# The tail of a graph network's layer 0 in chunks of 8, 4 and 10 tiles, with a table for each early place

## The chip, the cores and the metric

The kernel runs on one core of one Trainium2 chip. The metric is device time in microseconds (us) of a whole run. A core has five engines that run side by side, each with its own instructions in its own order: TensorE (PE, matrix products and transposes; PEld is its weight load), VectorE (DVE), ScalarE (ACT), GpSimd (POOL) and SyncE (SP), which only issues DMAs here. An engine waits for another one, or for a DMA, by a semaphore.

## The reference

Four graph layers over N = 2708 nodes with D = 128 features. The adjacency is sparse (8.0 neighbours a row on the mean) and all entries of one row are equal, so a row is known from one value and the places of its entries.

```
# layer 0: hyperbolic; every factor comes from row norms
h = h_add(h_mul(relu(layernorm(x)), embed), embed_bias)
neigh = exp_map_zero(adj @ log_map_zero(h))
x = x + h_add(h_mul(concat(relu(layernorm(x)), neigh), layer), layer_bias)
# layer 1: messages along edges
h = relu(layernorm(x));  s = h @ msg_w[:, :D].T;  d = h @ msg_w[:, D:].T
aggregated[i] = sum_j adj[i, j] * gelu(s[i] + d[j] + msg_b)
x = x + layernorm(gelu(concat(h, aggregated) @ upd_w.T + upd_b) + h) * ln_w + ln_b
# layers 2 and 3: products with adj and with weights
```

## The kernel before

**Tiles.** The nodes lie in T = 22 tiles of 128 (the last one has 20 rows), and the tiles in six blocks: 0 to 4 of four tiles, 5 of two. `first_half` is 12 tiles, blocks 0 to 2; the list `late` is blocks 3, 4 and 5.

**Layer 0.** For each block `read_block` loads a slab of the transposed adjacency in six pieces, and ACT makes a 0/1 mask of each (L999). From the masks come two things. The first is the product with all 22 tiles: 66 matmuls a block, three bf16 parts for each tile (`add_product`, L1324), and then the row norms (`end_product`, L1347). The second is the list of each row's neighbours: PE packs the mask into words (`words_in`, L1028, L1046), DVE takes the 24 largest words of a row (`find_words`, L1057 to L1072) and decodes them (`find_columns`), and POOL fetches one value for each row by an indirect DMA for each tile (L1120, `val`). `lay_out` sorts the neighbours of a half of the tiles into places: EARLY = 2 early places, HEAD - EARLY = 4 head places, and the rest into packed tail lists of NQ = 3 chunks a tile.

**The tail of layer 0** is a chain through small instructions: `neighbours` (row factors, the product with the layer's weights at L948, the sum at L1375, squares on ACT at L1383), then `update` (`norm`, `log_factor` and `moebius` on one column per tile, with two ACT table loads at L865 and L883; the new x at L1403 and L1408; `normal_form`, whose last instruction is returned as `formed`; then for each block h on ACT at L926, its transpose at L936, the product d with `msg_w` at L948, a copy to `v` at L1421 and DMAs to DRAM at L1424). It runs twice: for blocks 0 to 2, and for blocks 3 to 5. d goes to two tables in DRAM: `d_early` with the first 12 tiles' rows, and `d_hbm` with all.

**Order.** The framework orders each engine's instructions by their place in the program and by its own estimate of when each is ready. `queue_behind(ins)` adds an order by hand: an instruction stays behind `ins` on its engine. So the transposes of the first `update` stand behind the first 12 matmuls of product 4 (`last`), and the other 54 behind the last d matmul (`latest["times"]`); `find_words` of blocks 4 and 5 stands behind `formed`.

**The gathers.** POOL issues indirect DMAs that fetch a row of d for each of 128 nodes. `gather_early` (L1523) fetches both early places of 21 tiles, 42 gathers: a place whose neighbour is among the first 12 tiles reads `d_early`, and a miss is put with the tail. Its buffers are the three that the adjacency pieces used. `mark_edges` (L1237, L1240) and `pack_edges` (L1260 to L1306, one batch for each block, all behind the last d matmul) make the tail lists' indices `tail_c`.

**Layer 1's loop.** `prelude(g)` makes the node's own rows s (into `v`) and the update's own part for four tiles, and splits s into three bf16 parts (`split`, L783 to L786). Row t of the loop, `messages`, gathers 4 head places (`g`) and 3 tail chunks (`gt`, both L1727, from `d_hbm`, 4 buffers each), adds s, takes Gelu, sums on PE (L1787, L1789) and goes on to layer 1's end and layer 2's product (L1645). `prelude(0)` stands before the loop; the others go into its first rows. On-chip pools are stacked: `words`, `left`, `wide0`, `small` and others are closed before the loop, and the loop's pools lie where they lay.

Of the kernel before, what the change touches and what calls it, by code (L numbers as in the profile page):

```python
# [42 lines left out]
P = 128  # L43
# [513 lines left out]
def sparse_stack(  # L557
# [169 lines left out]

    d_hbm = dram.tile([NP + 1, D], F32, name="d_hbm")
    d_early = dram.tile([first_half * P + 1, D], F32, name="d_early")
# [18 lines left out]
    def load_later():  # L748

        nc.gpsimd.dma_start(out=d_hbm[NP : NP + 1, :], in_=none)  # L750
        nc.gpsimd.dma_start(out=d_early[first_half * P :, :], in_=none)
        for w, src in (
            (msg_w, msg_wt),
            (upd_w, upd_wt),
            (w2_w, w2),
            (self_w, w_self),
            (neigh_w, w_neigh),
        ):
            nc.gpsimd.dma_start(out=w, in_=src.rearrange("(a p) o -> p a o", p=P))
        for r, src in ((msg_br, msg_b), (upd_br, upd_b), (ln_wr, ln_w), (ln_br, ln_b)):  # L760
            nc.gpsimd.dma_start(out=r, in_=src.partition_broadcast(P))
# [25 lines left out]


# [7 lines left out]
    with ExitStack() as st:  # L796
# [14 lines left out]
        for t in range(T):  # L811
            nc.gpsimd.tensor_scalar_mul(shifts[:, t, :], ident, float(2 ** (T - 1 - t)))

# [22 lines left out]
        place = wide.tile([P, P], I32, name="place")  # L836
# [120 lines left out]
        def times_bias(w, bias, out, name):  # L957

            ps = ps_one.tile([P, BANK], F32, tag="one", name=f"wt{name}")
            nc.tensor.transpose(ps[:, :P], w, ident)  # L960
            wT = pair_p.tile([P, P], F32, tag="wT", name=f"wT{name}")
            nc.vector.tensor_copy(wT, ps[:, :P])
            nc.tensor.matmul(ps[:, P : P + 1], wT, bias, start=True, stop=True)
            nc.vector.tensor_copy(out, ps[:, P : P + 1])
# [57 lines left out]
        def pack(b):  # L1022
# [4 lines left out]
            for t in range(T):  # L1027
                nc.tensor.matmul(  # L1028
                    pk[:, :w], shifts[:, t, :], mask[:, t, sl], start=(t == 0), stop=(t == T - 1)
                )  # L1030
            return pk

        def words_in(b):
# [5 lines left out]
            pk = pack(b)  # L1039
# [87 lines left out]

        def lay_out(sl):
# [5 lines left out]
            from_c = float((T - first_half + 1) * P)  # L1134
# [4 lines left out]
            nc.vector.tensor_scalar(near, first[:, :, :EARLY], from_c, None, op0=ALU.is_ge)  # L1139
            nc.vector.scalar_tensor_tensor(  # L1140
                cand[:, sl, 2, SLOTS - EARLY :],
                first[:, :, :EARLY],
                from_c,
# [7 lines left out]
                -(from_c + first_half * P),  # L1151
# [4 lines left out]
            if sl.stop < T:  # L1156
                nc.vector.tensor_scalar_add(early_c[:, sl, :], miss, float(first_half * P))
# [92 lines left out]
        def pack_edges(b, after):  # L1250

            t0, t1 = blocks[b]
            n = t1 - t0
            px = ps_one.tile([P, BANK], F32, tag="one", name=f"ex{b}")
            px = px[:, : n * NQ * 32].rearrange("p (t q c) -> p t q c", t=n, c=32)
            for k in range(n):
                t = t0 + k
                for q in range(NQ):
                    with queue_behind(after):
                        nc.tensor.matmul(  # L1260
                            px[:, k, q, : TAIL + 3],
                            r_all[:, t, q * P : (q + 1) * P],
                            edge_x[:, t, :] if q < tails(t) else short_x,
                            start=True,
                            stop=True,
                        )
            ex = small.tile([P, BLOCK, NQ, TAIL + 3], F32, tag="ex", name=f"exs{b}")
            nc.scalar.copy(ex[:, :n], px[:, :, :, : TAIL + 3])  # L1268
            m = n * NQ
            kth, past, jump = (  # L1270
                small.tile([P, BLOCK * NQ], F32, tag=name, name=f"{name}{b}")[:, :m]
                for name in ("kth", "past", "jump")
            )
            flat_ex = ex.rearrange("p t q c -> p (t q) c")[:, :m, :]
            edge = small.tile([P, BLOCK, NQ], F32, tag="edge", name=f"edge{b}")[:, :n, :]
# [3 lines left out]
                tail_r[:, t0:t1, :].rearrange("p t q -> p (t q)"), flat_ex[:, :, TAIL + 2]  # L1279
            )  # L1280

            nc.vector.tensor_sub(kth, edge, flat_ex[:, :, TAIL])
            nc.vector.tensor_tensor(past, edge, flat_ex[:, :, TAIL + 1], ALU.is_ge)
            nc.vector.tensor_sub(jump, flat_ex[:, :, TAIL], flat_ex[:, :, TAIL + 1])
# [4 lines left out]
            sel = small.tile([P, BLOCK * NQ, TAIL], F32, tag="sel", name=f"sel{b}")[:, :m, :]  # L1289
# [6 lines left out]
            nc.vector.tensor_mul(sel, sel, flat_ex[:, :, :TAIL])  # L1296
            cf = small.tile([P, BLOCK * NQ], F32, tag="cf", name=f"cf{b}")[:, :m]
            nc.vector.tensor_reduce(cf, sel, AX.X, ALU.add)
            nc.vector.tensor_scalar_add(
                tail_c[:, t0:t1, :].rearrange("p t q -> p (t q)"), cf, MID  # L1300
            )
            if t1 == T:
                q = (n - 1) * NQ + tails(full)
                nc.vector.tensor_mul(sel[:, q, :HEAD], is_place, flat_ex[:, q, :HEAD])
                nc.vector.tensor_reduce(cf[:, q : q + 1], sel[:, q, :HEAD], AX.X, ALU.add)
                nc.vector.tensor_scalar_add(  # L1306
                    tail_c[:, full, tails(full) : tails(full) + 1], cf[:, q : q + 1], MID
                )
# [47 lines left out]
        def neighbours(bs, sums):  # L1356
# [3 lines left out]
            nc.vector.tensor_mul(n_sq, sums[0][:, : sl.stop - sl.start], val[:, sl])  # L1360
# [9 lines left out]
            for t0 in range(sl.start, sl.stop, 3):  # L1370
                g = slice(t0, min(t0 + 3, sl.stop))
                ps = tiles_times(g, yT, layer_w[:, 1, :], f"ne{t0}")
# [19 lines left out]
        def update(bs, copy, after):  # L1392
# [22 lines left out]
            for b in bs:  # L1415
# [6 lines left out]
                for table, end in ((d_early, first_half), (d_hbm, T)):  # L1422
# [96 lines left out]
        def gather_early(ts):  # L1519
            for t in ts:  # L1520
                n = rows(t)
                for k in range(EARLY):
                    nc.gpsimd.indirect_dma_start(  # L1523
                        out=early_d[t // EACH][:n, t % EACH, k, :],
                        out_offset=None,
                        in_=d_early,
                        in_offset=bass.IndirectOffsetOnAxis(ap=early_c[:n, t, k : k + 1], axis=0),
# [4 lines left out]
        sums = sums_of([0, 1, 2])  # L1532
# [10 lines left out]
        end_product(1, acc, sums)  # L1543
        lay_out(halves[0])
        with queue_behind(scaled):
            nc.vector.tensor_scalar(
                spread[:, : HEAD * rest].rearrange("p (k r) -> p k r", r=rest), apart, 0.0, None,
                op0=ALU.is_equal, saturate=False,
# [5 lines left out]
        find_words(3, words_in(3))  # L1554
        find_columns(groups[3])
        read_block(4)
        product(2, sums)
        neighbours([0, 1, 2], sums)
        read_block(5)
        sums = sums_of(late)  # L1560
        product(3, sums)
        words = {b: words_in(b) for b in (4, 5)}
        acc = begin_product(4)
        split_at = BLOCK
        last = add_product(4, acc, range(split_at))
        formed = update([0, 1, 2], nc.scalar.copy, last)
        find_words(4, words[4], formed)
# [5 lines left out]
        add_product(4, acc, range(split_at, T), latest["times"])  # L1573
# [4 lines left out]
        gather_early(range(first_half))  # L1578
# [5 lines left out]
        with queue_behind(last):  # L1584
            nc.vector.tensor_scalar_add(
                early_c[:, halves[1], :], late_c, float(first_half * P)
            )
        gather_early(range(first_half, full))
# [3 lines left out]
        for b in range(nb):  # L1592
            pack_edges(b, latest["times"])
# [98 lines left out]

    group_p = held.enter_context(tc.tile_pool(name="group", bufs=3))
    with ExitStack() as st_m:
        hot_p = st_m.enter_context(tc.tile_pool(name="hot", bufs=3))
        gath_p = st_m.enter_context(tc.tile_pool(name="gath", bufs=4))
        small = st_m.enter_context(tc.tile_pool(name="small1", bufs=2))
        junk_p = st_m.enter_context(tc.tile_pool(name="junk", bufs=1))

        def prelude(g):  # L1700

            sl = groups[g]
            n = sl.stop - sl.start
            for t in range(sl.start, sl.stop, 2):
                two = slice(t, min(t + 2, sl.stop))
                m = two.stop - t
                ps = ps_one.tile([P, BANK], F32, tag="one", name=f"own{t}")
                ps = ps[:, : m * 2 * D].rearrange("p (n j d) -> p n j d", j=2, d=D)
                for k in range(m):
                    nc.tensor.matmul(  # L1710
                        ps[:, k, :, :],
                        hT[:, (t + k) * P : (t + k + 1) * P],
                        pair_w[:, 0::2, :],
                        start=True,
                        stop=True,
                    )
                nc.vector.tensor_add(v[:, two, :], ps[:, :, 0, :], row_of(msg_br, m))
                left = group_p.tile([P, 2, D], F32, tag="left", name=f"lefts{t}", bufs=2)
                last = nc.vector.tensor_add(tmp[:, two, :], ps[:, :, 1, :], row_of(upd_br, m))
                split(v, two, left[:, :m, :])  # L1720
            with queue_behind(last):
                nc.vector.tensor_add(x[:, sl, :], x[:, sl, :], row_of(ln_br, n))
            return last
# [120 lines left out]
        first = prelude(0)  # L1844
# [5 lines left out]
        for t0, t1 in zip(starts, starts[1:] + [T]):  # L1850
# [3 lines left out]
            for k in range(n):  # L1854
# [6 lines left out]
                if begun < len(groups):  # L1861
                    prelude(begun)
# [194 lines left out]
```

## Time and profile before

| what | us |
|---|---|
| median of 3 runs | 555.48 (555.25 to 558.63) |
| the profiled execution, the whole run | 556.43 |
| its span | 554.6 |
| PE, DVE, ACT, POOL busy | 422.5, 419.9, 236.6, 234.7 |
| first early gather issued | 166.68 |
| last d copied to `v` | 204.19 to 204.56 |
| first head gather of the loop issued | 222.69 |
| last tail gather of the loop issued | 412.4 |

All times inside the span count from its start. An engine that is busy for three quarters of the span may still not set its end: layer 0 is mostly PE and DVE work, and the loop in the middle has POOL issuing gathers, so the stretches have to be read one by one. The busy shares of the page are for matmuls, vector work and POOL's indirect DMAs; issuing by SP isn't counted.

### The profile page before, as it was taken

To read this page: it belongs to the slowest core of one execution; us is meant where nothing else is said; L and a number is where in the kernel's file an instruction comes from. 1 tells how busy PE (TensorE), PEld (TensorE's weight loads), DVE (VectorE), ACT (ScalarE), POOL (GpSimd) and SP (SyncE) were. 2 spreads that over 40 slices of the span, in tenths; PEclk is the share of its full clock that TensorE was granted. 3 is DMA by queue.
4 is the path that set the end of the run, shared out by engine and by line. 5 is a ranking of instruction groups with operands and counts; after the bars stand their busy time and mean duration, and the time that the engine had idled before them with its cause. 6 is when DMAs were issued, how large, how long until landed. Compare 5 with 4: busy or idle time off the path is not lost.

```text
span 554.6 us, 8223 instructions
## 1 busy us (share of the span) xinstructions
PE 422.5 (76%) x2504; PEld 262.1 (47%) x2504; DVE 419.9 (76%) x1743; ACT 236.6 (43%) x570; POOL 234.7 (42%) x268
## 2 busy tenths in 40 slices
PE   0981999999993062276877968879877999989994
PEld 0760354464753051265646644646553555445652
DVE  6977986767998989437679786879546599998742
ACT  2867966766424131324535434454534344300100
POOL 8800022220047777777777777777760000000000
PEclk9996899999998555668888987989997999999998
DMA  8893779970031132123146473752220250399011
GB/s 260 278 318 124 227 248 331 305 210 2 1 115 43 52 96 52 48 52 104 51 151 203 153 206 101 232 170 52 54 47 2 83 219 1 116 390 394 20 57 51
DMA packets 39332, 77.89 MB, mean 140 GB/s; under 512 B 5754, under 2 KB 18614, under 8 KB 37722
## 3 DMA queue, kind: packets, MB, share of 16 engines
q1 hardware_dynamic: 30270, 63.15, 33.1%
q0 software_dynamic: 7264, 13.40, 9.6%
q10 hardware_dynamic: 1744, 0.72, 0.5%
q8 instruction: 22, 0.36, 0.3%
q14 instruction: 32, 0.26, 0.1%
HBM read 73.63 MB, written 3.62 MB: 139 GB/s over the span
## 4 chain that ended last, share of the span: by engine, by line
PE 37%; DVE 31%; DMA 12%; POOL 6%; issue 6%; ACT 5%; ACTq 0%; DVEq 0%
PE three L1645 8%; PE acc L1324 8%; PE two L1645 7%; DMA gt<-d_hbm,tail_c 5%; DMA a<-in_adj_t_dram 4%; POOL g L1727 4%; DVE eq L1661 3%; POOL gt L1727 3%; PE msg L1787 3%; DMA layer_w<-in_L_gnn_layer_dram 2%; PE d L948 1%; DMA hT<-in_adj_dram 1%; PE pk L1028 1%; DVE mask L994 1%; PE neigh L1684 1%
## 5 line engine op out<-in xcount | busy, mean ns | idle before, releaser
L1645 PEld LDWEIGHTS <-parts 128*128 128x128 bf16 x792 | 75.3, 101 | 90.4 <-issue 9.5
L1645 PE MATMUL two<-mask,parts 128*128 128x512 fp8e4 (+1 forms) x396 | 88.8, 381 | 9.3 <-ACT parts L1630 5.1
L1727 POOL DMA_INDIRECT g<-d_hbm,head_c x84 | 82.9, 986 | 25.8 <-issue 22.6
L1324 PE MATMUL acc<-mask,parts 128*128 128x512 fp8e4 (+1 forms) x396 | 79.6, 355 | 0.7 <-DVE parts L786 0.4
L1645 PE MATMUL three<-mask,parts 128*128 128x512 fp8e4 (+1 forms) x396 | 79.0, 354 | 0.6 <-ACT parts L1630 0.5
L1727 POOL DMA_INDIRECT gt<-d_hbm,tail_c x65 | 62.7, 964 | 19.8 <-issue 15.2
L1120 POOL DMA_INDIRECT val<-in_adj_dram,ai x22 | 22.0, 998 | 104.5 <-DVE left L1108 91.3
L1324 PEld LDWEIGHTS <-parts 128*128 128x128 bf16 x396 | 36.6, 98 | 47.6 <-ACT parts L783 7.5
L1523 POOL DMA_INDIRECT early<-d_early,early_c x42 | 43.0, 1023 | 12.8 <-issue 11.9
L999 ACT ACTIVATE mask<-a 128x2048 fp8e4<-128x2048 uint32 (+3 forms) x27 | 38.2, 1434 | 10.0 <-DMA a<-in_adj_t_dram 9.8
L1661 DVE TENSOR_SCALAR_CACHE_REDUCE eq<-row,val 128x2708 fp8e4<-128x2708 f32 (+1 forms) x13 | 39.4, 3031 | 2.4 <-DMA row<-in_adj_dram 2.3
L1028 PE MATMUL pk<-mask,shifts 128*128 128x512 fp8e4 (+1 forms) x132 | 31.1, 372 | 13.0 <-ACT mask L999 12.4
L1740 PE MATMUL msg<-parts,r_all 128*128 128x128 bf16 x195 | 15.7, 227 | 19.0 <-DVE u L1804 13.7
L1661 DVE TENSOR_SCALAR_CACHE_REDUCE eq<-hT,val 128x1354 fp8e4<-128x1354 f32 x18 | 29.1, 1619 | 0.1
L1787 PE MATMUL msg<-ident,early 128*128 128x128 f32 x84 | 16.4, 327 | 16.6 <-DVE gt L1776 13.3
L1776 DVE TENSOR_TENSOR gt<-gt,msg 128x384 f32<-128x384 f32 (+1 forms) x22 | 12.0, 545 | 21.5 <-DMA gt<-d_hbm,tail_c 19.1
L1710 PE MATMUL own<-pair_w,hT 128*128 128x256 f32 x44 | 15.9, 503 | 13.6 <-ACT exs L1268 9.6
L1787 PE MATMUL msg<-ident,g 128*128 128x128 f32 x168 | 25.5, 302 | 0.0
L926 ACT ACTIVATE h<-x,n_nb,n_rstd 128x128 f32<-128x128 f32 x44 | 18.2, 486 | 17.0 <-DVE n_nb L920 17.0
L1787 PEld LDWEIGHTS msg<-ident,g 128*128 128x128 f32 x168 | 24.2, 221 | 0.2
L1740 PEld LDWEIGHTS <-r_all 128*128 128x128 fp8e4 x195 | 13.5, 102 | 22.1 <-issue 18.0
L1773 DVE TENSOR_TENSOR g<-g,v 128x512 f32<-128x512 f32 x21 | 14.5, 689 | 11.3 <-DMA g<-d_hbm,head_c 11.3
(407 smaller groups left out, 867.2 us busy)
## 6 DMA issues: line engine op xcount, KB each, us to landing
a<-in_adj_t_dram SPq DMA_DIRECT2D x25, 1024.0 KB, 7.6
row<-in_adj_dram SPq DMA_DIRECT2D x12, 1354.0 KB, 9.6
hT<-in_adj_dram SPq DMA_DIRECT2D x18, 677.0 KB, 4.1
a<-in_adj_t_dram SPq DMA_DIRECT2D x5, 296.0 KB, 4.9
g<-d_hbm,head_c POOLq DMA_INDIRECT x84
a<-in_adj_t_dram SPq DMA_DIRECT2D x5, 256.0 KB
d_hbm<-v SPq DMA_DIRECT2D x5, 256.0 KB, 3.7
out_dram<-x SPq DMA_DIRECT2D x5, 256.0 KB
```

The lines of the kernel that those rows point to most:

```text
L926: nc.scalar.activation(h[:, t, :], x[:, t, :], AF.Relu, bias=node("nb")[:, t : t + 1], scale=node("rstd")[:, t : t + 1],)
L999: nc.scalar.activation(mask[:, g : g + n, sl], bits[:, :n, :w], AF.Sign, saturate=False)
L1028: nc.tensor.matmul(pk[:, :w], shifts[:, t, :], mask[:, t, sl], start=(t == 0), stop=(t == T - 1))
L1120: nc.gpsimd.indirect_dma_start(out=val[:, t : t + 1], out_offset=None, in_=flat, in_offset=bass.IndirectOffsetOnAxis(ap=ai[:, t : t + 1], ...
L1324: last = nc.tensor.matmul(acc[:, :w], parts[:, t, k, :], mask[:, t, sl], start=(t == 0 and k == 0), stop=(t == T - 1 and k == 2),)
L1523: nc.gpsimd.indirect_dma_start(out=early_d[t // EACH][:n, t % EACH, k, :], out_offset=None, in_=d_early, in_offset=bass.IndirectOffsetOnAx ...
L1645: last = nc.tensor.matmul(accs[b][:, : sl.stop - sl.start], parts[:, t, k, :], mask[:, t, sl], start=(t == 0 and k == 0), stop=(t == T - 1 ...
L1661: last = nc.vector.tensor_scalar(eq[:n, : c1 - c0], a, val[:n, t : t + 1], None, op0=ALU.is_equal, op1=ALU.add, accum_out=same[:n, t, k : ...
L1710: nc.tensor.matmul(ps[:, k, :, :], hT[:, (t + k) * P : (t + k + 1) * P], pair_w[:, 0::2, :], start=True, stop=True,)
L1727: nc.gpsimd.indirect_dma_start(out=g[:n, q, :], out_offset=None, in_=d_hbm, in_offset=bass.IndirectOffsetOnAxis(ap=table[:n, q : q + 1], a ...
L1740: nc.tensor.matmul(ps[:, q * D : (q + 1) * D], r_all[:, t, q * P : (q + 1) * P], parts[:, t, k, :], start=(k == 0), stop=(k == 2),)
L1787: nc.tensor.matmul(sums, part, ident, start=(q == 0), stop=False)
```

## The change

It does four things.

1. **Three chunks instead of two.** `neighbours` and `update` run for blocks 0 and 1 (8 tiles), for block 2 (4 tiles) and for `late` (10 tiles). The order of layer 0's tail is rewritten around this: product 3's first 12 matmuls go ahead of the first `update`'s transposes and its other 54 behind that update's last d matmul; the packing of words 4 and 5 goes behind product 3; product 4 is cut in the same way around `update([2])`.
2. **A table for each early place.** `reach` is [8 tiles, 12 tiles]. The first early place reads `d_early[0]`, the second `d_early[1]`. `lay_out` compares with a constant for each place (`from_c`, `none_c`). The 12 gathers of the first place for the first half are issued after `update([0, 1])`, the 12 of the second after the last values' gathers, and the 18 of the late tiles as before.
3. **Edges' packing in four batches**, blocks [0], [1, 2], [3, 4] and [5], with `prelude(0)` between the first and the second. `prelude` becomes a function of the whole kernel.
4. **Pools.** `gath` (buffers of `g` and `gt`) moves to the bottom of the loop's stack, ahead of `group`; `place` is allocated behind `shifts`; `wT` uses a `left` buffer.

```
+    reach = [groups[1].stop, first_half]
+    d_early = [dram.tile([n * P + 1, D], F32, name=f"d_early{n}") for n in reach]
...
+            nc.vector.tensor_tensor(near, first[:, :, :EARLY], each(from_c, n), ALU.is_ge)
...
-                for table, end in ((d_early, first_half), (d_hbm, T)):
+                for table, end in ((d_early[0], reach[0]), (d_early[1], reach[1]), (d_hbm, T)):
...
+        def times_layer(bs):
+            sl = slice(blocks[bs[0]][0], blocks[bs[-1]][1])
+            return {
+                t0: tiles_times(
+                    slice(t0, min(t0 + 3, sl.stop)), yT, layer_w[:, 1, :], f"ne{t0}"
+                )
+                for t0 in range(sl.start, sl.stop, 3)
+            }
...
-        sums = sums_of([0, 1, 2])
+        sums = sums_of([0, 1])
...
         end_product(1, acc, sums)
+        neighbours([0, 1], sums)
+        words = {3: words_in(3)}
+        read_block(4)
+        sums = sums_of([2])
+        product(2, sums)
+        times = times_layer([2])
+        acc = begin_product(3)
+        last = add_product(3, acc, range(BLOCK))
+        formed = update([0, 1], nc.scalar.copy, last)
+        through = latest["times"]
         lay_out(halves[0])
...
-        find_words(3, words_in(3))
+        neighbours([2], sums, formed, times)
+        find_words(3, words[3])
         find_columns(groups[3])
-        read_block(4)
-        product(2, sums)
-        neighbours([0, 1, 2], sums)
         read_block(5)
-        sums = sums_of(late)
-        product(3, sums)
-        words = {b: words_in(b) for b in (4, 5)}
-        acc = begin_product(4)
-        split_at = BLOCK
-        last = add_product(4, acc, range(split_at))
-        formed = update([0, 1, 2], nc.scalar.copy, last)
-        find_words(4, words[4], formed)
...
-        add_product(4, acc, range(split_at, T), latest["times"])
+        gather_early(range(first_half), [0])
+        sums = sums_of(late)
+        last = add_product(3, acc, range(BLOCK, T), through)
+        end_product(3, acc, sums)
+        words.update((b, words_in(b, last)) for b in (4, 5))
+        acc = begin_product(4)
+        last = add_product(4, acc, range(BLOCK))
+        formed = update([2], nc.scalar.copy, last)
+        through = latest["times"]
+        find_words(4, words[4], formed)
+        add_product(4, acc, range(BLOCK, T), through)
         end_product(4, acc, sums)
         find_words(5, words[5], formed)
         product(5, sums)
         find_columns(slice(groups[3].stop, T))
-        gather_early(range(first_half))
+        gather_early(range(first_half), [1])
         lay_out(halves[1])
...
-        gather_early(range(first_half, full))
+        gather_early(range(first_half, full), range(EARLY))
...
-        for b in range(nb):
-            pack_edges(b, latest["times"])
+        through = latest["times"]
+        packed = pack_edges([0], through)
+        first = prelude(
+            0,
+            ps_one,
+            lambda t, m: left_p.tile([P, BLOCK, D], F32, tag="left", name=f"lefts{t}")[:, :m, :],
+            packed,
+        )
+        pack_edges([1, 2], through)
+        pack_edges(late[:2], through)
+        pack_edges(late[2:], through)
...
+    gath_p = held.enter_context(tc.tile_pool(name="gath", bufs=4))
     group_p = held.enter_context(tc.tile_pool(name="group", bufs=3))
...
-        first = prelude(0)
```

In `pack_edges` the matmuls and ACT's copies stay one for each block; the eleven DVE instructions after them work on all blocks of a batch at once, in buffers of twice the size. `neighbours` takes an `after` (its first instruction goes behind `formed`) and ready products `times`.

## The prediction

> **What bounds the kernel now.** I first read the busy time of each engine by stretches (us from the span's start; columns: length, PE, PEld, DVE, ACT, POOL busy, clock, DMA share, GB/s).
>
> ```profile
> 98.00:125.00 27.00, 26.25 (x144) 14.58 (x144) 18.67 (x122) 19.13 (x21) 7.78 (x9) 1.00 0.81 258
> 125.00:145.00 20.00, 19.96 (x114) 10.40 (x113) 16.39 (x97) 10.91 (x38) 0.00 (x0) 1.00 0.01 1
> 145.00:158.00 13.00, 12.83 (x121) 10.12 (x120) 12.66 (x78) 8.78 (x21) 0.00 (x0) 1.00 0.29 86
> 158.00:182.00 24.00, 13.81 (x80) 8.12 (x77) 21.09 (x130) 7.40 (x28) 18.59 (x18) 0.86 0.19 51
> 223.00:410.00 187.00, 139.91 (x900) 99.72 (x898) 133.31 (x475) 81.47 (x244) 142.49 (x147) 0.87 0.40 119
> ```
>
> PE is full from 98 to 158, and POOL idle from 125 to 158. POOL's timeline then shows where its work begins and how it goes on (start, duration, idle time before in brackets).
>
> ```profile
> 158.23 0.95 POOL L1120 DMA_INDIRECT val<-in_adj_dram,ai  x1 [38.48 <-DVE left L1108]
> ...
> 166.68 1.35 POOL L1523 DMA_INDIRECT early<-d_early,early_c  x1 [0.30 <-issue]
> 168.33 0.95 POOL L1523 DMA_INDIRECT early<-d_early,early_c  x1 [0.30 <-issue]
> ...
> 221.21 0.95 POOL L1523 DMA_INDIRECT early<-d_early,early_c  x1 [0.31 <-issue]
> 222.69 1.04 POOL L1727 DMA_INDIRECT g<-d_hbm,head_c  x1 [0.53 <-ACT parts L783]
> 224.03 0.95 POOL L1727 DMA_INDIRECT g<-d_hbm,head_c  x1 [0.30 <-issue]
> ```
>
> From 158.23 POOL issues 6 value gathers, 42 early ones and 149 of the loop with about 0.30 us between them: a gather costs 0.95 + 0.30 = 1.25 us, and the loop's 149 take 187 us, from 222.7 to 410. So **from 158 to 410 POOL's queue sets the pace**, and moving its first loop gather moves the end. Last, the chain of waits around 222: it does not run through the early gathers but through the edges' packing.
>
> ```profile
> 221.71 0.06 DVE tail_c L1306
> 221.77 0.04 issue
> 221.82 0.43 DVE v L1717
> 222.28 0.41 ACT parts L783
> 222.69 1.03 POOL g L1727
> ```
>
> Thus two queues end together: POOL's early gathers (222.16) and DVE's six batches of packing (206.94 to 221.77), on whose memory the loop's `g` buffers lie. Taking away one alone would gain nothing.
>
> **What the Trainium skill says.** "TensorE: Matmul & The Clock Gate", section on the array's architectural detail, calls ACT and DVE strict first-in-first-out, and GpSimd too. The trace agrees for POOL: the first half's columns were ready at 99.4 and its last `d_early` write was issued at 156.94, yet the first early gather waited to 166.68, behind the values. "ScalarE: Activation LUTs", section on what a table load costs, says 1283 ns for each; the trace has 1.28 us. "DMA: Bandwidth & Descriptors", section on issuing engines, says that DMAs of all engines interleave on the same 16 DMA engines, so a change of place costs little but issue time; between 125 and 145 the DMA share is 0.01, so the moved gathers meet nothing there.
>
> **The change, part by part.**
>
> *POOL's queue.* The 42 early gathers took 55.5 us (166.68 to 222.16), 1.32 each. Twelve go ahead of 158: 15.9 us into the 33 us in which POOL idles. They need 8 tiles' d (worked out below: in DRAM by about 136), `early_c`, and the adjacency's buffers, whose last mask was made at 129. So they run about 136 to 152. What stays takes 6 values and 30 gathers, and ends at 222.2 - 15.9 = 206.3, plus the delay of the last `find_columns`. A word block's padding (a memset of 0.2 us on POOL) may stand behind them to 152; words 5 aren't needed before 157.
>
> *The packing's hold on the buffers.* The loop's `g` buffers now lie over `words` and `left`, those of `gt` over `shifts` and `place` (2 x 2048 + 2 x 2048 and 5632 + 512 bytes a partition, against 4 x 2048 and 4 x 1536). All but `left` are done with the words at about 160; `left` goes free with `prelude(0)`, and serves rows 2 and 3. So the first gather needs `d_hbm`: last copy to `v` ended 204.56, its DMA issued at 204.6, landing 3.7 us later: 208.3. **POOL's end (206.3) and d's landing (208.3) replace 222.7.** Undelayed, the gain is 222.7 - 208.3 = 14.4.
>
> *Row 0's tail indices* came at 209.5 after the first batch, and its `gt` gathers go out four gathers after the first: no wait. The rest of DVE: a batch has some 0.9 us of small instructions and 1.5 of large ones; four batches, two of them double, save 3 us of 14.9, and `prelude(0)` (5 us, 221.8 to 226.7) goes between. DVE so reaches row 0 near 223 plus the delay below, when its first `gt` has landed (before: 233.3). POOL may run four rows (35 us) ahead by its 4 buffers: no stall.
>
> *The delay of d.* This is the cost. PE has no idle time before 168, and the first `update` now comes inside that. PE's arrival: product 3 began at 122.0, its 12 matmuls take 2.6, so 124.6. The chain of blocks 0 and 1 starts when their norms are there, 98.95. For 12 tiles it took from 120.33 to 147.5, 27.2 us; for 8 it loses four squares (1.3) and a group of x (2.9): 23.0, so 122. But ACT is shared with block 4's masks (1.91 each, 19.13 of 27 us busy), and the chain passes ACT five times (tanh, squares, Ln, tanh, h), waiting half a mask or so each time: 4.5 taken, `formed` at 126.5. Two groups of transposes and d at 2.86 each (three took 147.56 to 156.13) reach 132.2. Of these 7.6 us PE works 2.9 on the groups, and product 4's first 12 matmuls, which stand behind nothing, fill 2.6: 2.1 lost. Products `ne` of block 2 hold two of four PSUM buffers, `nsq` a third, so transposes and d take turns: two copies of 0.6, 1.2 lost. The second update has 4 tiles and its chain ends (some 16 us after 126.5) long before PE comes to it at about 152: 0. Two more DMA issues on SP (0.36 to 0.5, behind block 5's pieces) and three short DVE memsets: 0.2. **Sum: 3.5 us later**, with 0 and 8.3 as ends: 0 if masks step aside and the fills are whole; 3.5 + 2.6 + 2.2 = 8.3 without the fill and with half as much ACT queueing again.
>
> *An added chain* is some 81 DVE instructions of 0.16 at intervals of 0.08 to 0.2, 8 to 13 us, and up to three table loads (3.8 us). DVE had 8.3 us free in 98 to 125 and 3.6 in 125 to 145, so about 12; words 3, `find_columns` and `lay_out` lose their idle gaps but nobody waits before 145. If that cover is gone, the words 4 and 5 wait: they already come with PE 3.5 later, so POOL ends at 209.8, still ahead of d's 211.8.
>
> *Comparisons with two constants* cost the same 0.17 us. The first place misses more often (counted over the inputs, 123 rows against 28, and the fullest tile has 377 of 384 tail slots), which adds no instruction, as chunks are fixed.
>
> *The sum.* The first gather goes at 208.3 + 3.5 + 0.3 of issue = 212.1, against 222.7: 10.6 less. The loop is POOL's from there on, so its end moves as much. Span 554.6 - 10.5 = 544.1; with the 1.8 around it 545.9 for the profiled run, which stood 0.95 above the median: **545.0**.
>
> **Rivals.**
>
> *The first row is still tied to the packing* (a buffer's release that I place wrongly, or `tail_c` awaited as a whole). Then the gathers start after DVE's packing and prelude: 222 + 3.5 less 3 saved = 222.5, or 219 in parts. Time 552 to 555.5. For it: in the trace before that was the last wait. Against: bytes add up exactly as above, and `val` was read by parts (a `neighbours` at 120.33 while tile 15's value was fetched at 118.60).
>
> *Slower: PE held behind `through`.* ACT and DVE work strictly in order, and `update` stands in the program after `read_block(4)`. If ACT's order puts all of block 4's masks (the last at 117.2) ahead of the squares, `formed` comes 16.9 us later, at 134.1; if DVE's puts `lay_out`, words 3 and their columns (some 14 us) ahead of it too, at 148. PE then loses 154 - 124.6 - 2.9 - 2.6 = 23.9, with 1.2 as above 25 us. The gathers start at 233.7, 11 later: 566. It decides from a delay of 14.4 (no gain) and of 20 (slower by 1%). Against: the order is by readiness, and DVE filled gaps out of program order in this trace.
>
> *The early gathers don't move*: the first place's 12 find their d or buffers late, after 152, and values queue behind them. POOL has 48 gathers, 62 us, so ends by 216 to 222: 549 to 555.
>
> **How the numbers follow.** My forecast 0.75 (delay 0 to 8.3: 541 to 549.5), tied to the packing 0.11, slower 0.10, gathers unmoved 0.04. The range takes in the forecast with its bounds, 0.5 below it, and the two rivals of little gain: 540 to 556, leaving out about 0.14. One per cent is 5.55 us, about what a measurement here can tell from no change. Faster by more: 0.75 and a part of the last rival, 0.76; within: 0.14; slower: 0.10.
>
> **What would show it.** Right: 12 early gathers between 125 and 158; the first `g` gather at 209 to 216, its wait ended by the `d_hbm` write; DVE's packing running beside gathers; POOL without gaps to about 399. PE's idle time between 122 and 175 is the delay: 2 to 6 us. Wrong: the first `g` gather behind `tail_c` or `parts`; PE idle for 10 us or more before the first transposes; a gap in POOL's queue in rows 4 to 8 for want of buffers.

## The result, and the profile after

The changed kernel takes 573.68 us (median of 4 runs, 572.4 to 575.28), against 556.21 for the kernel before on the same chip: 1.0303 times the time, 95% interval 1.0273 to 1.0332. It is slower by 3.0%, where 545.0 and faster had been predicted. The span of the profiled execution is 571.2 us, 16.6 more than before.

The loop's first head gather shows where this sits. It had gone at 222.69 and was predicted for 212.1; it went at 238.25, 15.6 later than before. From it to the last tail gather the loop takes 190.5 us (238.25 to 428.71), against 189.7 before (222.69 to 412.39). So 15.6 of the 16.6 us lie ahead of the loop. These are the same stretches as those shown of before (length, PE, PEld, DVE, ACT, POOL busy, clock, DMA share, GB/s):

```profile
98.00:125.00 27.00, 26.80 (x141) 14.14 (x142) 25.34 (x181) 24.39 (x42) 7.56 (x8) 1.00 0.81 251
125.00:145.00 20.00, 14.91 (x60) 8.59 (x59) 13.45 (x99) 11.19 (x29) 1.89 (x3) 0.74 0.28 83
145.00:158.00 13.00, 12.97 (x73) 6.66 (x72) 11.29 (x47) 3.19 (x7) 10.56 (x9) 1.00 0.17 42
158.00:182.00 24.00, 22.92 (x180) 15.60 (x178) 16.08 (x100) 3.95 (x9) 13.90 (x15) 1.00 0.19 53
223.00:410.00 187.00, 127.44 (x843) 91.73 (x843) 134.53 (x476) 76.90 (x227) 131.22 (x134) 0.84 0.38 114
```

POOL does work between 125 and 158 now, as meant. But between 125 and 145 PE has 14.91 of 20 us where it had 19.96, and its clock fell to 0.74; its work stretches on into 158 to 182 (22.92 busy, 13.81 before). POOL's timeline (start, duration, and in brackets the idle time before and what ended it) has the rest:

```profile
142.50 0.94 POOL L1577 DMA_INDIRECT early<-d_early,early_c  x1 [19.99 <-DMA d_early<-v]
...
159.11 1.43 POOL L1577 DMA_INDIRECT early<-d_early,early_c  x1 [0.30 <-issue]
160.54 0.20 POOL L1080 MEMSET wt<- 128x108 f32 x1
167.13 0.95 POOL L1577 DMA_INDIRECT early<-d_early,early_c  x1 [6.39 <-issue]
...
177.25 0.94 POOL L1158 DMA_INDIRECT val<-in_adj_dram,ai  x1 [0.30 <-issue]
...
216.85 1.11 POOL L1577 DMA_INDIRECT early<-d_early,early_c  x1 [0.30 <-issue]
238.25 0.97 POOL L1781 DMA_INDIRECT g<-d_hbm,head_c  x1 [20.29 <-DVE tail_c L1346]
```

Three things are to be seen. The early gathers end at 218, but then POOL stands for 20.29 us before the loop's first gather. The wait that the profile names is the packing's `tail_c`, as before. And eight early gathers of the second place (167.13 to 176.95) now run ahead of the six late value gathers (177.25 to 184.44), which had gone first. Ahead of the first loop gather, the chain of waits (start, us, what) reads:

```profile
237.56 0.18 DVE tail_c L1346
237.75 0.50 issue
238.25 0.97 POOL g L1781
```

The late tiles' chain shows the second loss. It starts at the first `n_nsq` of the ten late tiles. DVE's timeline of the kernel before, then of the changed one:

```profile
170.18 0.17 DVE L1360 TENSOR_TENSOR n_nsq<-nsq,val 128x10 f32<-128x10 f32 x1 [1.30 <-PE nsq L1347]
```

```profile
186.64 0.17 DVE L1411 TENSOR_TENSOR n_nsq<-nsq,val 128x10 f32<-128x10 f32 x1 [6.53 <-DMA val<-in_adj_dram,ai]
```

It is 16.5 us late. The last 6.5 of them DVE stood for the values, so PE's row norms came some 10 us late (about 180.1) and the values another 6.5. After that the chain ran as before and a little faster: the last copy of d to `v` ended at 219.27, 14.7 later than before. PE's timeline has the start of this:

```profile
130.59 1.63 PE L969 MATMUL hTpm<-ident,h 128*128 128x128 f32 x4 [3.74 <-ACT h L959]
132.89 2.07 PE L981 MATMUL d<-pair_w,hT 128*128 128x128 f32 x8 [0.67 <-ACT hT L970]
134.75 1.06 PE L969 MATMUL hTpm<-ident,h 128*128 128x128 f32 x4
136.49 2.08 PE L981 MATMUL d<-pair_w,hT 128*128 128x128 f32 x8 [0.67 <-ACT hT L970]
```

PE stood 3.74 us for the first `update`'s h, and what followed ran slowly: eight d matmuls took 2.07 us, which take 1.16 at full clock.

So there were three theories. **Theory 1**: the first gather waits until every tile of the pools that lay under `gath` is free, not only those whose bytes it takes. **Theory 2a**: PE is held behind the first update's d. **Theory 2b**: the values stand in POOL's queue behind the second place's gathers. The rivals: the wait is for data (`tail_c`, d), or the batches and the prelude cost the time and not the chunks.

### The profile page after: what moved, and what is told of

It reads as the page before. It is cut to its first block, busy times and chain, and to the rows that moved or that the text cites. A ratio compares the mean times of both kernels' runs of the same rounds, so it can differ in the third digit from the quotient of the medians.

```text
span 571.2 us, 8298 instructions
## 1 busy us (share of the span) xinstructions
PE 423.8 (74%) x2504; PEld 263.1 (46%) x2504; DVE 424.1 (74%) x1805; ACT 239.5 (42%) x576; POOL 239.0 (42%) x269
## 4 chain that ended last, share of the span: by engine, by line
DVE 23%; PE 22%; POOL 10%; issue 9%; DMA 6%; ACT 3%; DVEq 0%; ACTq 0%
PE three L1720 8%; PE two L1720 7%; DMA gt<-d_hbm,tail_c 4%; POOL g L1781 4%; POOL gt L1781 3%; DVE eq L1736 3%; POOL early L1577 3%; PE msg L1841 2%; PE neigh L1759 1%; DVE gt L1830 1%; DVE r_all L1280 1%; PE self L1759 1%; DMA g<-d_hbm,head_c 1%; DMA hT<-in_adj_dram 1%; PE own L801 1%
## 5 line engine op out<-in xcount | busy, mean ns | idle before, releaser
L1720 PE MATMUL two<-mask,parts 128*128 128x512 fp8e4 (+1 forms) x396 | 86.4, 372 | 9.4 <-ACT parts L1705 5.6
L1364 PE MATMUL acc<-mask,parts 128*128 128x512 fp8e4 (+1 forms) x396 | 81.4, 363 | 0.4 <-DVE parts L789 0.4
L1577 POOL DMA_INDIRECT early<-d_early,early_c x42 | 45.7, 1088 | 42.0 <-DMA d_early<-v 20.0
L969 PE MATMUL hTpm<-ident,h 128*128 128x128 f32 x22 | 6.4, 400 | 26.1 <-ACT h L959 26.1
L1827 DVE TENSOR_TENSOR g<-g,v 128x512 f32<-128x512 f32 x21 | 14.5, 689 | 14.7 <-DMA g<-d_hbm,head_c 14.7
L1841 PEld LDWEIGHTS msg<-ident,early 128*128 128x128 f32 x84 | 13.4, 224 | 24.6 <-DVE gt L1830 20.6
```

What stands on the lines that cost most here:

```text
L1364: last = nc.tensor.matmul(acc[:, :w], parts[:, t, k, :], mask[:, t, sl], start=(t == 0 and k == 0), stop=(t == T - 1 and k == 2),)
L1577: nc.gpsimd.indirect_dma_start(out=early_d[t // EACH][:, t % EACH, k, :], out_offset=None, in_=d_early[k], in_offset=bass.IndirectOffsetOn ...
L1720: last = nc.tensor.matmul(accs[b][:, : sl.stop - sl.start], parts[:, t, k, :], mask[:, t, sl], start=(t == 0 and k == 0), stop=(t == T - 1 ...
L1841: nc.tensor.matmul(sums, part, ident, start=(q == 0), stop=False)
```

## The experiments

Ratios are to the kernel before, on the same chip and in the same comparison; "late chain" is the first `n_nsq` of the late tiles. All kernels but e_pack_2 start from the changed one. Profiles differ by up to 2.5 us in when layer 0 gets to this stage (PE's stall ahead of the first d ends at 128.12 in ab_2 and at 130.59 in the changed kernel), so a difference of that size in a time column says nothing.

| kernel | edits | late chain | first `g` | median | ratio (95%) |
|---|---|---|---|---|---|
| before | | 170.18 | 222.69 | 556.21 | 1 |
| changed | | 186.64 | 238.25 | 573.68 | 1.0303 (1.0273 to 1.0332) |
| h_isplace | `is_place` elsewhere | 186.00 | 229.34 | 566.17 | 1.0158 (1.0107 to 1.0208) |
| a_pool | A: pools | 185.31 | 223.16 | 559.48 | 1.0037 (1.0017 to 1.0057) |
| b_vals | B: values first | 178.16 | 231.08 | 568.48 | 1.0216 (1.0180 to 1.0252) |
| c_nohold | C: product 3 free | 184.48 | 237.32 | 572.60 | 1.0296 (1.0254 to 1.0337) |
| ab_2 | A, B | 177.64 | 215.99 | 553.91 | 0.9941 (0.9918 to 0.9965) |
| abc | A, B, C | 177.50 | 216.40 | 554.86 | 0.9955 (0.9939 to 0.9971) |
| abd | A, B, D (padding on DVE) | 179.03 | 219.19 | 554.68 | 0.9941 (0.9918 to 0.9964) |
| abcd_2 | A, B, C, D | 170.75 | 209.65 | 544.84 | 0.9795 (0.9743 to 0.9847) |
| e_pack_2 | before + parts 3, 4 | 168.37 | 221.69 | 558.02 | 1.0008 (0.9987 to 1.0029) |
| f_chunks_2 | parts 1, 2 alone | 186.36 | 237.44 | 573.33 | 1.0290 (1.0244 to 1.0336) |

The four kernels whose names end in _2 had run once before, under the same expectations, on a chip on which the kernel before itself took 624 to 654 us. The ratios there were A and B 1.001 (0.995 to 1.007), all four 0.987 (0.976 to 0.998), parts 3 and 4 alone 1.035 (0.996 to 1.073), and none for parts 1 and 2 alone. None contradicts the table, and no other figure here is from there.

**One tile moved.** `is_place` does not lie under a buffer of `g` or `gt`: as built, these take exactly the bytes of `words`, `left`, `shifts` and `place`, and `is_place` starts 512 bytes a partition behind their end. In the changed kernel only the last packing batch reads it (L1344), not every one as the expectation has it, and that read ends 0.9 us before the gather.

```diff
-        is_place = wide.tile([P, HEAD], F32, name="is_place")
+        is_place = const.tile([P, HEAD], F32, name="is_place")
```

> One edit to the changed kernel: the tile `is_place`, which every packing batch reads, is allocated in a pool that stays open, nothing else. In the changed kernel the loop's first `g` gather goes at 238.25, 0.5 us after the last packing batch has read `is_place`. Theory 1 (the gather waits for the release of every tile of the pools under `gath`, whether its bytes lie under the buffer or not): the next latest releases are `left` by DVE in prelude(0) at 228.1 and `short_x` by PE at 225.8, so the first `g` gather goes at about 228.5, 10 us earlier, span about 561. Rival (the gather waits for `tail_c` itself, or for d): nothing moves, first gather 238, span 571.

Measured: first gather at 229.34, 8.9 earlier, and a ratio that falls from 1.0303 to 1.0158. In DVE's timeline of this kernel the last reader of `left` is where theory 1 puts the next wait:

```profile
228.10 0.42 DVE L789 TENSOR_TENSOR parts<-lefts,parts 128x256 bf16<-128x256 f32 x1
```

And POOL's timeline:

```profile
229.34 1.30 POOL L1781 DMA_INDIRECT g<-d_hbm,head_c  x1 [12.04 <-DVE early L1827]
```

The instructions of the packing are the same and three of its four batches still come after this gather; only the pool that one tile belongs to has changed. So the gather did not wait for data; the wait on the pool stands. The waits written into the built programs say the same: the changed kernel's first gather has one on the read of `is_place`, which in this kernel has become one on this read of `left`. That the profile names `early` (L1827) here is a case of a wait for several things put down to whichever came last.

**The pools (A).**

```diff
+        old = st.enter_context(tc.tile_pool(name="old0", bufs=1))
-        shifts = wide.tile([P, T, P], BF16, name="shifts")
+        shifts = old.tile([P, T, P], BF16, name="shifts")
-        place = wide.tile([P, P], I32, name="place")
+        place = old.tile([P, P], I32, name="place")
...
-            lambda t, m: left_p.tile([P, BLOCK, D], F32, tag="left", name=f"lefts{t}")[:, :m, :],
+            lambda t, m: tmp[:, 16 + t : 16 + t + m, :],
```

> Two edits to the changed kernel: `shifts` and `place` get a pool of their own, so that `gath` lies over pools whose tiles are all free early, and prelude(0)'s split writes its scratch into unused rows of `tmp` instead of `left`. Theory 1 (release of whole pools): the first `g` gather waits only for d in DRAM, landing at 222.3, so it goes at about 222.6 instead of 238.25 and the time falls by 15.5 to about 558 (span 555.7). Rival (`tail_c` or d itself holds it): 238 and 573 as in the changed kernel.

POOL's timeline:

```profile
215.33 1.11 POOL L1578 DMA_INDIRECT early<-d_early,early_c  x1 [0.30 <-issue]
223.16 0.94 POOL L1782 DMA_INDIRECT g<-d_hbm,head_c  x1 [6.71 <-DMA d_hbm<-v]
```

The gather now waits for d in DRAM, and for nothing else that ends late, while three of the four packing batches end later than 240. The time is back at that of the kernel before, within half a per cent (1.0037).

**The values first (B).**

```diff
-                        nc.gpsimd.indirect_dma_start(
+                        fetched = nc.gpsimd.indirect_dma_start(
...
+            return fetched
...
-        find_columns(slice(groups[3].stop, T))
-        gather_early(range(first_half), [1])
+        fetched = find_columns(slice(groups[3].stop, T))
+        with queue_behind(fetched):
+            gather_early(range(first_half), [1])
```

> One edit to the changed kernel: the 12 second-place early gathers stand behind the 6 late value gathers on POOL, by an order written out. In the changed kernel 8 of them ran from 167.1 to 177.0 ahead of the values, and the chain of the late tiles then waited 6.5 us for `val` at 186.64. Theory 2b: `n_nsq` of `late` comes 6.4 us earlier, at 180.2, and with it the chain to the end of the packing; first `g` gather at 231.9, time about 567 (span 564.8). Rival: the late chain is held by PE or DVE all the same and moves by less than 2 us; time 572 to 574.

POOL's timeline:

```profile
168.74 0.95 POOL L1158 DMA_INDIRECT val<-in_adj_dram,ai  x1 [10.24 <-DVE left L1146]
...
174.99 0.94 POOL L1158 DMA_INDIRECT val<-in_adj_dram,ai  x1 [0.30 <-issue]
176.24 0.94 POOL L1578 DMA_INDIRECT early<-d_early,early_c  x1 [0.30 <-issue]
```

The late chain starts at 178.16, no longer behind the values but behind PE's row norms; the first gather goes 7.2 earlier and the ratio falls to 1.0216. POOL now idles 10 us ahead of the values, and the kernel is faster for it.

**Product 3 set free (C).**

```diff
-        last = add_product(3, acc, range(BLOCK, T), through)
+        last = add_product(3, acc, range(BLOCK, T))
```

> One edit to the changed kernel: the rest of product 3 (54 matmuls) no longer stands behind the last d matmul of the first update. Theory 2a (PE stood 3.7 us and then ran the first update's transposes and d at half clock, about 8 us lost in all, because the rest of product 3 had to wait for them): PE has no idle time between 122 and 135, reaches the late row norms up to 8 us earlier, but `val` then still comes behind the early gathers; first `g` gather between 231 and 238, time 566 to 573. If d of the first update comes later for it, the early gathers start later and the values may wait more: up to 576. Rival (PE isn't what delays the late chain): first gather unchanged at 238, time 573.

This one is a null in time (1.0296), and the rival's number. Its PE timeline says why that is not the rival's reason:

```profile
132.17 1.13 PE L981 MATMUL d<-pair_w,hT 128*128 128x128 f32 x8
133.14 0.60 PE L969 MATMUL hTpm<-ident,h 128*128 128x128 f32 x4
133.57 1.03 PE L1364 MATMUL acc<-mask,parts 128*128 128x512 fp8e4 x4
134.46 1.16 PE L981 MATMUL d<-pair_w,hT 128*128 128x128 f32 x8
...
155.10 0.48 PE L1084 MATMUL wp<-ident,wt 128*128 128x128 f32 x1 [7.76 <-POOL wt L1080]
```

The hold was real: without it product 3's matmuls fill the waits, d runs at full clock (1.13 and 1.16), and the packing of words 4 begins at 138.72 instead of 151.18. But then PE stands 7.76 us before the transpose of words 5, for a memset of 0.2 us on POOL that stands behind the 12 early gathers. In the changed kernel PE came there so late that this same wait was 1.0 us. Behind the 7.76 us PE's clock was at 0.51 for 2.9 us more (155.1 to 158), which takes back about 1.4 (an estimate: half of 2.9). The values too, still behind the second place's gathers, held the late chain to 184.48 here, so they covered the same gain a second time.

**A and B together.** 

> The two edits that moved the time so far, together on the changed kernel: the pools (`shifts` and `place` in a pool of their own, prelude(0)'s scratch in `tmp`) and the second-place early gathers behind the late value gathers. If the two losses are separate and add up: late chain 7 us earlier than with the pools alone, so d lands at about 216 and the first `g` gather goes at about 216.3 (with the pools alone 223.16), span about 550.7, time about 552.5. If POOL's own queue becomes the bound (its early gathers end at 215), the same within 1 us. If the losses overlap: about 558 as with the pools alone.

First gather at 215.99 and 553.91 us, near what adding up gave (216.3 and 552.5): the two losses lie one after the other on the path.

**All four.** D moves the padding of words 5 off POOL.

```diff
-                nc.gpsimd.memset(wt[:, w : n * P], 0.0)
+                nc.vector.memset(wt[:, w : n * P], 0.0)
```

> On top of those two edits: the rest of product 3 not behind the first update's d, and the memset that pads the words of block 5 on DVE instead of POOL. Where product 3's rest alone was set free, PE finished product 3 at 138.9 instead of 151.2, then stood 7.76 us before the transposes of words 5, whose padding POOL made only after 12 early gathers (147.3 to 155.1). Theory 3 (the memset stands in POOL's queue): PE doesn't stand there, the late row norms come at about 170 as in the kernel before (170.2), the values are fetched at 157 to 166, d lands at about 208.5, first `g` gather at about 209, span about 541, time about 543. Rival (something else keeps the late chain, such as DVE finding and sorting neighbours): first `g` gather at 213 to 216, time 547 to 552.

Windows of this kernel (same columns), then POOL's timeline:

```profile
125.00:145.00 20.00, 19.72 (x107) 10.33 (x106) 15.09 (x107) 11.98 (x31) 3.48 (x4) 1.00 0.31 89
```

```profile
208.38 0.96 POOL L1579 DMA_INDIRECT early<-d_early,early_c  x1 [0.30 <-issue]
209.65 1.08 POOL L1784 DMA_INDIRECT g<-d_hbm,head_c  x1 [0.30 <-issue]
```

PE is full and at full clock while POOL works beside it, and from 160.43 to the loop POOL has no gap: its own queue is the bound, and the first gather follows the last early one by 0.30 us. This version takes 544.84 us, 2.05% less than the kernel before (1.5 to 2.6), and beats both.

**C and D apart.** Is the 9 us between ab_2 and abcd_2 C's or D's?

> Pools, values first, and the rest of product 3 set free, with the padding of words 5 left on POOL. If the memset behind POOL's 12 early gathers takes back what the freed product gives: PE stands some 7 to 8 us before the transposes of words 5, until the last of the 12 early gathers at about 155, late row norms at about 177, first `g` gather at about 213 to 215 (215.99 without the freed product), time 550 to 553. If the freed product is the whole gain: first `g` gather at 209.7, time 545.

> Pools, values first, and the padding of words 5 on DVE, with the rest of product 3 held behind the first update's d as in the changed kernel. If the hold costs by itself: PE stands 3.7 us at 128 and runs the transposes and d at half clock, saves only the 1.0 us wait for the memset; first `g` gather at about 215, time 552 to 554. If the memset was the whole cost: first `g` gather at 209.7, time 545.

It is neither's alone: 554.86 and 554.68, against 553.91 without both. With C alone, PE stands as in c_nohold (PE's timeline of abc):

```profile
153.25 0.48 PE L1085 MATMUL wp<-ident,wt 128*128 128x128 f32 x1 [7.76 <-POOL wt L1081]
```

With D alone, PE stands behind the hold and loses its clock (PE's timeline of abd):

```profile
129.89 1.63 PE L970 MATMUL hTpm<-ident,h 128*128 128x128 f32 x4 [3.73 <-ACT h L960]
132.19 2.08 PE L982 MATMUL d<-pair_w,hT 128*128 128x128 f32 x8 [0.68 <-ACT hT L971]
```

The hold and the memset are two waits, and PE loses nearly as much with either: with D alone some 9 us to the hold and the clock behind it (summed below), with C alone 7.76 to the memset and about 1.4 to the clock. Only where both are gone is the time gained.

**The parts of the change apart.** e_pack_2 is the kernel before with parts 3 and 4 of the change (the batches, `prelude`, the pools) and nothing else; f_chunks_2 is the changed kernel with these two parts undone. Of its edit, the calls of the packing:

```diff
-        packed = pack_edges([0], through)
-        first = prelude(
...
-        pack_edges([1, 2], through)
-        pack_edges(late[:2], through)
-        pack_edges(late[2:], through)
+        for b in range(nb):
+            pack_edges(b, latest["times"])
```

> The kernel before with parts 3 and 4 of the change alone: the packing in four batches with prelude(0) after the first, and the pools moved; the layer's tail in two chunks as before. If the chunks are what delays the late chain (theories 2a and 2b): packing begins at 206.9 as before, ends about 222.4 with prelude(0) inside it, first `g` gather at about 223 behind the last batch, time 555 to 557, no change. If the batches or the prelude cost the loss: first `g` gather at 230 to 238, time 563 to 573.

> The changed kernel with the packing and pools of the kernel before: parts 1 and 2 alone (three chunks, a table for each early place). If the chunks cost the loss: packing begins at about 222.5, ends at 237.5, first `g` gather at about 238.3, time 571 to 575. If the batches cost it: 555 to 560.

Parts 3 and 4 alone change nothing (1.0008): POOL's timeline has the first gather at once behind the early ones.

```profile
220.44 0.94 POOL L1549 DMA_INDIRECT early<-d_early,early_c  x1 [0.30 <-issue]
221.69 1.07 POOL L1741 DMA_INDIRECT g<-d_hbm,head_c  x1 [0.30 <-issue]
```

Parts 1 and 2 alone cost what the whole change costs (1.0290, first gather 237.44). The rival that blames the batches falls. The hold is in e_pack_2 too, as it is in the kernel before; it costs time only where the packing comes late.

## Why the prediction was wrong

Its sum had the first gather at 212.1. It went at 238.25, 26.2 later. That is 15.1 from the hold on the buffers (238.25 against 223.16 in a_pool, where it is gone) and 11.1 from d: its landing came 14.0 late where 3.5 was predicted (222.3 in a_pool against 208.3), and from landing to gather it took 0.85 us where 0.3 had been taken.

**"The packing's hold on the buffers" failed, as a mechanism.** The prediction counted bytes: `g` over `words` and `left`, `gt` over `shifts` and `place`, so that only d's landing was left. The bytes were right. But `shifts` and `place` belong to `wide0`, as `is_place` does, and the last packing batch reads `is_place` at 237.2. One tile in another pool brought the gather to 229.34, and pools of which every tile is free early brought it to 223.16. This was in the profile of before: the first gather there waited for the end of packing too. The prediction read this as a matter of bytes ("on whose memory the loop's `g` buffers lie"), but as built the packing's working tiles lie behind the last byte of `g` and `gt` there too; they share pools with tiles that lie under them.

**"The delay of d" failed, in size and in what it left out.** Three terms:

- *PE behind `through`*. Predicted 2.1 of waiting, 1.2 of PSUM turns, 0.2: 3.5. Measured: 3.74 of waiting (126.84 to 130.59, since `formed` ended at 130.01 and not at 126.5), 1.34 of turns (0.67 twice), and a term that was missing: half clock. Between 130.59 and 138.57 the two groups' transposes and d took 6.84 where they take 3.52 at full clock (twice 0.60 and 1.16): 3.3. Of this the clock took 2.3 (0.91 on each d, 0.46 on the second transposes); the first transposes (1.63) also waited for ACT's h, five of which took 2.03. The clock stayed at 0.50 until 140.67, so that product 3's matmuls lost about 1.05 more (an estimate: half of 2.1). Together 9.4. "TensorE: Matmul & The Clock Gate" of the Trainium skill, in its part on the clock gate, says that PE drops to half clock after an idle window of about 3.4 us; the trace agrees (3.74 idle, then 2.07 against 1.16).
- *The second update and the words: 0*. The memset was named ("may stand behind them to 152; words 5 aren't needed before 157") and costed at nothing. It cost 1.0 here, since the gathers lasted to 160.5, and 7.76 once PE was early. With the 9.4 this covers the 10.1 that PE's row norms came late.
- *The values: 0*. They were said to wait on words 4 and 5 alone. In fact eight second-place gathers stood ahead of them, and the late chain waited 6.5 for values. "What stays takes 6 values and 30 gathers" added up POOL's time, but never asked in which order.

That `formed` was late was ACT's queue, which the prediction named and sized too small (4.5 for all five passes). ACT's timelines, of the changed kernel and then of the kernel before:

```profile
109.97 1.91 ACT L1032 ACTIVATE mask<-a 128x2048 fp8e4<-128x2048 uint32 x1
...
113.31 1.89 ACT L1032 ACTIVATE mask<-a 128x2048 fp8e4<-128x2048 uint32 x1
115.11 0.19 ACT L899 ACTIVATE n_lm<-n_nl 128x8 f32<-128x8 f32 x1
115.20 2.41 ACT L1032 ACTIVATE mask<-a 128x2048 fp8e4<-128x2048 uint32 x2
...
119.45 0.21 ACT L916 ACTIVATE n_e<-n_t 128x8 f32<-128x8 f32 x1
```

```profile
132.59 0.20 ACT L866 ACTIVATE n_lm<-n_nl 128x12 f32<-128x12 f32 x1
...
134.10 0.21 ACT L883 ACTIVATE n_e<-n_t 128x12 f32<-128x12 f32 x1
```

From DVE's `n_nl` to the end of `n_e` the chain took 10.5 us (109.18 to 119.66), against 1.9 before (132.43 to 134.31): five masks, 6.8 us, stood between its steps, and two table loads of 1.28 that had run ahead of their data before now stood on the path.

**"POOL's queue"** was right that 12 gathers fit into the idle stretch, but they ran 142.5 to 160.5 instead of 136 to 152, behind the late d. POOL's end was 218.0, not 206.3 plus 3.5; with A, B, C and D it was 209.3, and 209.8 was the predicted sum.

**"Row 0's tail indices"** were right: where the gathers start ahead of the packing, POOL doesn't stand for them. **"An added chain"** was right that DVE had room: 25.34 of 27 us busy between 98 and 125 where 18.67 were before, and the late words waited for PE. ACT had less, 24.39 where 19.13 were before. That the constants cost nothing was not tried by itself. A slip in the sum changes nothing: delays of 0 to 8.3 give 541.5 to 549.8, not 541 to 549.5.

**The rivals.** "Still tied to the packing" had the mechanism, given 0.11 and priced with the small delay, so that it ended at 552 to 555.5. "Held behind `through`" had the direction, given 0.10; it named a delay of 14.4 as the point of no gain. The delay was 14.0, and a_pool, which has the delay without the tie, measured 1.0037: that point was right. Its cause as given came true in part: ACT's masks did stand in the chain, but they put `formed` at 130.0 and not at 134.1 or 148, and the clock, the memset and the values made up the rest. The two were set out as alternatives; both came true at once, and their sum is the result. No chance had been given to that.

The gain predicted was there to be had: with the ties undone the first gather goes at 209.65 (212.1 predicted) and the time is 544.84 (545.0). That is another kernel than the one predicted, and doesn't make the prediction right. The agreement of the time is luck besides, as the gather went 2.5 us earlier than predicted and what follows took that much longer.

## What to carry to other kernels

Where a late stage's buffers lie over closed pools, ask which tile of those pools is read last, not which bytes are taken; a constant in the wrong pool can hold a whole stage. When work is moved into an engine's idle time, write down what stands behind it in that queue, down to a 0.2 us memset, and who waits for that. And when an edit that takes a visible wait away gives nothing, look at the next wait in the new trace before dropping the idea: two waits side by side have to go together.

## What the hardware showed that was not expected

An idle time of 3.74 us on PE cost nearly as much again afterwards (2.3 and about 1.05 us): the granted clock was 0.50 from 130.43 to 140.67, over the whole dependent run of transposes and d and 2 us into product 3's matmuls. With product 3's matmuls in the waits, PE never stood there and the same d took 1.13 and 1.16 us. How long the clock stays low is not settled by the wait before it. In a_pool PE stood 3.72 us in the same place and had the same two short waits (0.68 each), but its clock was at 0.50 for 6.8 us only (128.4 to 135.2), and its second d ran at full clock:

```profile
131.84 2.08 PE L982 MATMUL d<-pair_w,hT 128*128 128x128 f32 x8 [0.68 <-ACT hT L971]
...
135.45 1.16 PE L982 MATMUL d<-pair_w,hT 128*128 128x128 f32 x8 [0.68 <-ACT hT L971]
```

So the short waits alone did not keep the clock low; why it stayed low longer in the changed kernel is open.
